# Two scans, then two gates: the order of VectorE's work in a selective-scan step

## Chip, cores and metric

The kernel runs on one core of a Trainium2 chip. The metric is the device time of one execution in microseconds; the median of three runs before the change is 5415.38 us (5413.15 to 5421.7). A core has five engines that run side by side, each taking its own instructions strictly in order and waiting on semaphores for the others: TensorE (PE, matmuls and transposes), VectorE (DVE), ScalarE (ACT), GpSimd (POOL) and SyncE (SP, which gives out most of the transfers here).

## What is computed

Sixteen sequences of 512 positions and 256 features go through a bidirectional selective state-space layer (a Mamba block), a layer norm, a mixture of soft experts and another layer norm. The part that matters here is the recurrence, which runs forward and backward, for 512 channels and 16 states each:

```python
def _selective_scan(u, dt, A, B, C, D, reverse=False):
    dA = jnp.einsum('bld,dn->bldn', dt, A)
    dB_u = jnp.einsum('bld,bld,bln->bldn', dt, u, B)
    ...
    dA_shift = jnp.pad(dA[:, 1:], ((0, 0), (0, 1), (0, 0), (0, 0)))
    dA_cum = jnp.exp(jnp.flip(jnp.cumsum(jnp.flip(dA_shift, 1), 1), 1))
    xs = jnp.cumsum(dB_u * dA_cum, 1) / (dA_cum + 1e-12)
    y = jnp.einsum('bldn,bln->bld', xs, C)
    ...
    return y + u * D
```

The kernel writes `xs` as a recurrence h[t] = exp(dt[t] A) h[t-1] + (dt u B)[t], times a factor that stands for the 1e-12 in the denominator, 0.5 (1 + tanh(...)). The product with C and the sum over states follow; the halves are taken into the weights beforehand.

## The kernel before

Channels lie on the 128 partitions in four chunks, the 512 positions along the free dimension. For each sequence `scan_part` (L392) is called four times: forward and backward, each for two of the four chunks. Within a call a loop runs over pairs of states (n = 0, 2, ..., 14) and the two chunks of the call. One turn of the inner loop is called a step here; there are 16 in a call and 1024 in all. A step does the following:

- SyncE loads `bs` and `cs`, the B and C rows of the two states, broadcast to all partitions (L416, L417, once for both chunks).
- GpSimd multiplies `du` by `bs` into `db` (L427), for both states at once.
- ScalarE computes the decay of each state with an exp (L444) and its factor `th` with a tanh (L446). The decay goes into a PSUM bank of its own, called `h`, which the scan then overwrites with its result.
- VectorE runs the recurrence of each state with a scan (L450 forward, L452 backward), and forms the gate (L455) `hg = (th + 1) * h` for each state.
- GpSimd multiplies both states' `hg` by `cs` in one instruction (L456).
- TensorE transposes `hg` and adds it up in the accumulator `acc` (L371), two steps later.

In 256 of the steps (n = 4 and 12) the second state's input comes from TensorE instead (`by_diagonal`, L405): a matmul puts it into a bank of the common PSUM pool, called `hd`, and the decay goes to an SBUF tile `dec`. The scan then overwrites `hd`. Such steps are called single here, the other 768 double.

Buffers set how far an engine may run ahead: `db` has three, `hg` four, `th` three, and the PSUM pool of `h` three banks (L97). So the exp of a state waits for the gate of the state three before it, which is the last reader of that bank; `th` has the same depth. A db product waits for the scans of the step three before it.

Besides the steps, generators give out pieces of other work: preparation of the next sequence, projections, norms, the experts of sequences already scanned. `beside_scan` (L541) takes some pieces at the end of each step. They use all engines; a piece is often a short run of VectorE and ScalarE instructions.

The order on each engine is not simply the order of the program text. A planner (the framework's) keeps its own clock and gives each engine, of the instructions it takes to be ready, the one that comes first in the program. `late(...)` pins an instruction behind the one written before it on its engine; most pieces of other work begin with such an instruction, while scans, gates, exps and tanhs are not pinned. The order so found is fixed in the built program.

Of the kernel before, what the change touches and what calls it, by code (L numbers as in the profile page):

```python
# [12 lines left out]
ALU = mybir.AluOpType  # L13
# [42 lines left out]
def seq_layers(tc, ident, neghalf, a, out):  # L56
# [20 lines left out]
    nc = tc.nc  # L77
    nb = a["x"].shape[0]
    with ExitStack() as ctx:
# [27 lines left out]
        def bank(name):  # L107
            count[0] += 1
            if tail and count[0] % 8 >= 3:
                return tail[0].tile([P, 512], F32, tag="tps", name=name)  # L110
            return ps.tile([P, 512], F32, tag="mps", name=name)
# [15 lines left out]
        def late(ins):  # L127

            return tc.keep_in_program_order(ins)
# [212 lines left out]
        def turn_pair(b, r, p, v):  # L342

            yield 2
            pts = []
            for c in (2 * p, 2 * p + 1):
                pt = bank(f"pdu_{b}_{r}_{c}")
                for lc in range(NL):
                    s = slice(lc * P, (lc + 1) * P)
                    nc.tensor.transpose(pt[:, s], v[c][2][:, s], ident)  # L350
                pts.append((c, pt))
            yield HOLD
            for c, pt in pts:
                duT = p4.tile([P, L], F32, tag="duT", name=f"duT_{b}_{r}_{c}", bufs=2)
                late(nc.scalar.copy(duT, pt))
                v[c].append(duT)
# [4 lines left out]
        def add_up(depth):  # L361
            while len(pending) > depth:
                first, unit, last, c, hc, accs, w, u, name, done = pending.pop(0)
                if first:
                    accs[c] = ps_acc.tile([P, L], F32, tag="acc", name=name)

                    late(nc.tensor.matmul(accs[c], zeros[:, :P], zeros, start=True, stop=False))
                for j in range(2):
                    for lc in range(NL):
                        s = slice(lc * P, (lc + 1) * P)  # L370
                        ins = nc.tensor.matmul(  # L371
                            accs[c][:, s],
                            hc[:, j, s],
                            ident,
                            is_transpose=True,
                            start=False,
                            stop=(last and j == 1 and lc == NL - 1),
                        )
                        if j == lc == 0:
                            late(ins)  # L380
                if unit:
                    for lc in range(NL):
                        s = slice(lc * P, (lc + 1) * P)
                        nc.tensor.matmul(accs[c][:, s], u[:, c, s], w["diagD"][:, c, :], start=False, stop=False)
                if last:
                    evictions.append(partial(done, c))

        def evict():
            while evictions:
                evictions.pop(0)()  # L390

        def scan_part(b, r, p, v, accs, done, then):  # L392

            prep.drain()
            prep.gens += [[1, g] for g in [turn_pair(b, r, p, v)] + then]
            w = side[r]
            made = {}

            def by_diagonal(n, c):

                diags.append(count[0])
                made[n, c] = h = bank(f"hd_{b}_{r}_{n}_{c}")
                for lc in range(NL):
                    s = slice(lc * P, (lc + 1) * P)
                    ins = nc.tensor.matmul(h[:, s], v[c][3][:, s], dg[:, s], start=True, stop=True)  # L405
                    if lc == 0:
                        late(ins)

            chunks = (2 * p, 2 * p + 1)
            for n in range(0, NS, 2):  # L410
                q = f"{b}_{r}_{p}_{n}"
                k = 1 if n + 1 in DIAG else 2

                bs = p4.tile([P, 2, L], F32, tag="bs", name=f"bs_{q}")
                cs = p4.tile([P, 2, L], F32, tag="cs", name=f"cs_{q}")
                nc.sync.dma_start(bs[:, :k, :], v["bc"][0, n : n + k, :].unsqueeze(0).to_broadcast([P, k, L]))  # L416
                nc.sync.dma_start(cs, v["bc"][1, n : n + 2, :].unsqueeze(0).to_broadcast([P, 2, L]))  # L417
                if n + 3 in DIAG:
                    dg = p4.tile([P, L], F32, tag="dg", name=f"dg_{q}", bufs=1)
                    nc.sync.dma_start(  # L420
                        dg.rearrange("p (l s) -> p l s", l=NL),
                        diag_dram[r, DIAG.index(n + 3), :, : P * P].rearrange("l (p s) -> p l s", p=P),
                    )
                for c in chunks:
                    dt, rr, du = v[c][:3]
                    db = p4.tile([P, 2, L], F32, tag="db", name=f"db_{q}_{c}")
                    nc.gpsimd.tensor_tensor(  # L427
                        db[:, :k, :], du.unsqueeze(1).to_broadcast([P, k, L]), bs[:, :k, :], ALU.mult
                    )
                    hg = p4.tile([P, 2, L], F32, tag="hg", name=f"hg_{q}_{c}", bufs=4)  # L430
                    hs = {}
                    for j in range(2):
                        if j < k:
                            dec = h = ps_h.tile([P, L], F32, tag="h", name=f"h_{q}_{c}_{j}")
                            hs[j] = (h, dec, db[:, j, :])
                        else:
                            h = made.pop((n + j, c))
                            dec = p4.tile([P, L], F32, tag="dec", name=f"dec_{q}_{c}", bufs=2)
                            hs[j] = (h, dec, h)

                    ths = {}
                    for j in range(2) if k == 2 else (1, 0):
                        s = slice(n + j, n + j + 1)
                        nc.scalar.activation(hs[j][1], dt, AF.Exp, scale=w["A"][:, c, s])  # L444
                        ths[j] = p4.tile([P, L], F32, tag="th", name=f"th_{q}_{c}_{j}")
                        nc.scalar.activation(ths[j], rr, AF.Tanh, bias=LN_1E12 / 2, scale=w["Ah"][:, c, s])  # L446
                    for j in range(2):
                        (h, dec, add), th = hs[j], ths[j]
                        if r == 0:
                            nc.vector.tensor_tensor_scan(h, dec, add, 0.0, ALU.mult, ALU.add)  # L450
                        else:
                            nc.vector.tensor_tensor_scan(  # L452
                                h[:, ::-1], dec[:, ::-1], add[:, ::-1], 0.0, ALU.mult, ALU.add
                            )
                        nc.vector.scalar_tensor_tensor(hg[:, j, :], th, 1.0, h, ALU.add, ALU.mult)  # L455
                    nc.gpsimd.tensor_tensor(hg, hg, cs, ALU.mult)  # L456
                    pending.append(
                        (r == n == 0, n == 0, r == 1 and n == NS - 2, c, hg, accs, w, v["u"], f"acc_{q}_{c}", done)
                    )
                    evict()  # L460

                    nxt_n = n if c == chunks[0] else n + 2
                    if nxt_n + 1 in DIAG:
                        for x in sides:
                            x.take_up()
                        by_diagonal(nxt_n + 1, chunks[1] if c == chunks[0] else chunks[0])
                    beside_scan()
                    if k == 1:
                        diags.pop(0)
                    add_up(2)  # L470
# [70 lines left out]
        def beside_scan():  # L541
            for x in sides:
                x.take_up()
            prep.piece()
            for x in (front, back) if front.credit > back.credit else (back, front):
                x.paced_piece(gaps=not hurry)
# [549 lines left out]
```

## Time and profile before

| | us |
|---|---|
| median of three runs | 5415.38 |
| the profiled execution | 5411.23 |
| its span in the trace | 5409.4 |
| busy: GpSimd, VectorE, TensorE matmul, ScalarE | 4732, 4560, 4331, 4087 |
| VectorE: scans (L450, L452) with h | 2144 in 1792 |
| VectorE: scans with hd | 312 in 256 |
| VectorE: gates (L455) | 1359 in 2048 |
| GpSimd: db (L427), hg (L456) | 2144, 2421 |
| ScalarE waits for a gate: L446, L444 | 331, 218 |

How to read the views. The page's first part gives each engine's busy time; the second cuts the span into 40 slices with the busy share of each in tenths. The groups list instructions by line and shape: out<-in, count, then total busy time, mean length in ns, then the idle time of the engine just before them and what ended most of it. A line of the waits names who waited, for whom, the total, the number of waits and the longest. A line of the timeline is a start, a length, the engine, the line and the tiles, with xN where N instructions in a row are merged. Recorded lengths of neighbours on one engine can overlap a little, so the distance between starts (the pitch) is what adds up: 1.13 us for a scan followed by something that doesn't wait for it, 0.59 us for a gate.

### The profile page before, as it was taken

To read this page: it belongs to the slowest core of one execution; us is meant where nothing else is said; L and a number is where in the kernel's file an instruction comes from. 1 tells how busy PE (TensorE), PEld (TensorE's weight loads), DVE (VectorE), ACT (ScalarE), POOL (GpSimd) and SP (SyncE) were. 2 spreads that over 40 slices of the span, in tenths; PEclk is the share of its full clock that TensorE was granted. 3 is DMA by queue.
4 is the path that set the end of the run, shared out by engine and by line. 5 is a ranking of instruction groups with operands and counts; after the bars stand their busy time and mean duration, and the time that the engine had idled before them with its cause. 6 is when DMAs were issued, how large, how long until landed. Compare 5 with 4: busy or idle time off the path is not lost. (4 is left out here: it accounts for less than half of the span.)

```text
span 5409.4 us, 73721 instructions
## 1 busy us (share of the span) xinstructions
PE 4331.1 (80%) x24144; PEld 3390.0 (63%) x24145; DVE 4559.7 (84%) x6276; ACT 4087.2 (76%) x6515; POOL 4732.1 (87%) x2537
## 2 busy tenths in 40 slices
PE   5656666898888978788888977889787897888889
PEld 3445555676666666677656765667656776667657
DVE  7888988889898899888998888988899889988722
ACT  6677777787888778887877887788788887877641
POOL 6999999999999899998999989998999989988600
PEclk7778778898899988899888989899889998989999
DMA  4334333575446644566446754467444764457436
GB/s 137 131 117 137 125 129 131 189 230 159 156 142 212 225 149 148 158 223 213 131 144 194 232 170 153 132 212 232 149 149 146 225 224 134 145 179 234 126 103 188
DMA packets 595236, 907.73 MB, mean 168 GB/s; under 512 B 78082, under 2 KB 384898, under 8 KB 594852
## 3 DMA queue, kind: packets, MB, share of 16 engines
q1 hardware_dynamic: 521156, 859.87, 49.5%
q10 hardware_dynamic: 73696, 43.14, 2.8%
q8 instruction: 192, 3.15, 0.2%
q14 instruction: 192, 1.57, 0.1%
HBM read 840.86 MB, written 62.01 MB: 167 GB/s over the span
## 5 line engine op out<-in xcount | busy, mean ns | idle before, releaser
L456 POOL TENSOR_TENSOR hg<-hg,cs 128x1024 f32<-128x1024 f32 x1024 | 2420.8, 2368 | 128.1 <-DVE hg L455 110.0
L427 POOL TENSOR_TENSOR db<-du,bs 128x1024 f32<-128x1024 f32 (+1 forms) x1024 | 2144.4, 2098 | 232.3 <-DVE h L450 84.7
L371 PE MATMUL acc<-ident,hg 128*128 128x128 f32 x8192 | 1179.3, 295 | 203.3 <-POOL hg L456 181.6
L455 DVE SCALAR_TENSOR_TENSOR hg<-th,h 128x512 f32<-128x512 f32 x1792 | 1185.8, 678 | 177.2 <-PE acc L371 90.4
L371 PEld LDWEIGHTS acc<-ident,hg 128*128 128x128 f32 x8192 | 1044.9, 154 | 390.8 <-POOL hg L456 240.9
L452 DVE TENSOR_TENSOR_SCAN h<-h,db 128x512 f32<-128x512 f32 x896 | 1072.8, 1218 | 112.2 <-ACT h L444 107.5
L450 DVE TENSOR_TENSOR_SCAN h<-h,db 128x512 f32<-128x512 f32 x896 | 1071.1, 1217 | 48.8 <-ACT h L444 45.7
L446 ACT ACTIVATE th<-rr,Ah_f 128x512 f32<-128x512 f32 x1024 | 725.0, 714 | 186.3 <-DVE hg L455 183.1
L446 ACT ACTIVATE th<-rr,Ah_b 128x512 f32<-128x512 f32 x1024 | 721.5, 712 | 155.2 <-DVE hg L455 147.7
L444 ACT ACTIVATE h<-dt,A_f 128x512 f32<-128x512 f32 x896 | 608.2, 680 | 117.5 <-DVE hg L455 112.6
L444 ACT ACTIVATE h<-dt,A_b 128x512 f32<-128x512 f32 x896 | 608.6, 681 | 108.8 <-DVE hg L455 105.1
L687 PE MATMUL pl<-x2T,seT 128*128 128x512 f32 x512 | 299.1, 715 | 78.7 <-DVE hg L455 37.4
L405 PE MATMUL hd<-dg,duT 128*128 128x128 f32 x2048 | 305.6, 298 | 32.7 <-ACT yt L627 13.5
L830 PEld LDWEIGHTS pg<-st,Wg 128*128 128x128 f32 x2048 | 244.8, 196 | 106.2 <-issue 85.0
L405 PEld LDWEIGHTS hd<-dg,duT 128*128 128x128 f32 x2048 | 283.1, 214 | 38.4 <-ACT yt L627 15.7
L806 PE MATMUL peo<-Wd,ht 128*128 128x256 f32 x1024 | 257.0, 407 | 55.6 <-DVE rr L337 38.6
L779 PE MATMUL pu<-st,Wu 128*128 128x128 f32 x2048 | 254.5, 283 | 50.1 <-DMA Wu<-in_Wu_dram 32.7
L962 PE MATMUL cpo<-ceo,ct 128*128 128x256 f32 x1024 | 254.8, 407 | 46.9 <-DVE rr L337 39.9
L779 PEld LDWEIGHTS pu<-st,Wu 128*128 128x128 f32 x2048 | 244.9, 198 | 61.5 <-DVE h L452 24.2
L830 PE MATMUL pg<-st,Wg 128*128 128x128 f32 x2048 | 269.9, 286 | 4.1 <-DMA Wg<-in_Wg_dram 3.1
L884 PE MATMUL cl<-seT,cx 128*128 128x512 f32 x512 | 244.7, 617 | 32.5 <-DVE res L272 12.3
L806 PEld LDWEIGHTS peo<-Wd,ht 128*128 128x128 f32 x1024 | 205.3, 206 | 97.7 <-DVE rr L337 41.2
(154 smaller groups left out, 6654.8 us busy)
## 6 DMA issues: line engine op xcount, KB each, us to landing
cs<-bc SPq DMA_DIRECT2D x512, 512.0 KB, 3.9
bs<-bc SPq DMA_DIRECT2D x384, 512.0 KB, 5.1
Wg<-in_Wg_dram SPq DMA_DIRECT2D x128, 512.0 KB, 6.0
Wu<-in_Wu_dram SPq DMA_DIRECT2D x128, 512.0 KB, 6.0
Wd<-in_Wd_dram SPq DMA_DIRECT2D x128, 512.0 KB, 5.5
dg<-diag_dram SPq DMA_DIRECT2D x128, 256.0 KB, 4.2
bs<-bc SPq DMA_DIRECT2D x128, 256.0 KB, 3.6
x<-in_x_dram SPq DMA_DIRECT2D x32, 512.0 KB, 6.3
```

The source lines that it names most:

```text
L371: ins = nc.tensor.matmul(accs[c][:, s], hc[:, j, s], ident, is_transpose=True, start=False, stop=(last and j == 1 and lc == NL - 1),)
L405: ins = nc.tensor.matmul(h[:, s], v[c][3][:, s], dg[:, s], start=True, stop=True)
L427: nc.gpsimd.tensor_tensor(db[:, :k, :], du.unsqueeze(1).to_broadcast([P, k, L]), bs[:, :k, :], ALU.mult)
L444: nc.scalar.activation(hs[j][1], dt, AF.Exp, scale=w["A"][:, c, s])
L446: nc.scalar.activation(ths[j], rr, AF.Tanh, bias=LN_1E12 / 2, scale=w["Ah"][:, c, s])
L450: nc.vector.tensor_tensor_scan(h, dec, add, 0.0, ALU.mult, ALU.add)
L452: nc.vector.tensor_tensor_scan(h[:, ::-1], dec[:, ::-1], add[:, ::-1], 0.0, ALU.mult, ALU.add)
L455: nc.vector.scalar_tensor_tensor(hg[:, j, :], th, 1.0, h, ALU.add, ALU.mult)
L456: nc.gpsimd.tensor_tensor(hg, hg, cs, ALU.mult)
L779: nc.tensor.matmul(pu[:, fc * P : (fc + 1) * P], got["Wu", e][:, k, fc * P : (fc + 1) * P], st[:, k, :, j * SL : (j + 1) * SL], start=(k = ...
L806: nc.tensor.matmul(po[:, j * DM : (j + 1) * DM], ht[:, fc, :], got["Wd", e0 + j][:, fc, :], start=(fc == 0), stop=(fc == NF - 1),)
L830: nc.tensor.matmul(pg[:, fc * P : (fc + 1) * P], got["Wg", e][:, k, fc * P : (fc + 1) * P], st[:, k, :, j * SL : (j + 1) * SL], start=Fals ...
```

## The change

The loop that gave out scan and gate of each state in turn is split into two loops: both scans first, then both gates. The operations, their operands and buffers are the same.

```diff
                     for j in range(2):
-                        (h, dec, add), th = hs[j], ths[j]
+                        h, dec, add = hs[j]
                         if r == 0:
                             nc.vector.tensor_tensor_scan(h, dec, add, 0.0, ALU.mult, ALU.add)
                         else:
                             nc.vector.tensor_tensor_scan(
                                 h[:, ::-1], dec[:, ::-1], add[:, ::-1], 0.0, ALU.mult, ALU.add
                             )
-                        nc.vector.scalar_tensor_tensor(hg[:, j, :], th, 1.0, h, ALU.add, ALU.mult)
+                    for j in range(2):
+                        nc.vector.scalar_tensor_tensor(hg[:, j, :], ths[j], 1.0, hs[j][0], ALU.add, ALU.mult)
                     nc.gpsimd.tensor_tensor(hg, hg, cs, ALU.mult)
```

## The prediction

> **What bounds the kernel now.** I read the page's busy line and slices first, then its costliest groups, then the waits of GpSimd and VectorE between 300 and 4950 us (the part with the steps in full swing), and last VectorE's timeline.
>
> ```profile
> span 5409.4 us, 73721 instructions
> PE 4331.1 (80%) x24144; PEld 3390.0 (63%) x24145; DVE 4559.7 (84%) x6276; ACT 4087.2 (76%) x6515; POOL 4732.1 (87%) x2537
> ...
> DVE  7888988889898899888998888988899889988722
> ...
> POOL 6999999999999899998999989998999989988600
> ```
>
> GpSimd (POOL) is busiest, and its last slices are empty: the last step's product ends at 5132 us. Then comes a tail of 277 us without steps, in which the change has nothing to move.
>
> ```profile
> L456 POOL TENSOR_TENSOR hg<-hg,cs 128x1024 f32<-128x1024 f32 x1024 | 2420.8, 2368 | 128.1 <-DVE hg L455 110.0
> L427 POOL TENSOR_TENSOR db<-du,bs 128x1024 f32<-128x1024 f32 (+1 forms) x1024 | 2144.4, 2098 | 232.3 <-DVE h L450 84.7
> ...
> L455 DVE SCALAR_TENSOR_TENSOR hg<-th,h 128x512 f32<-128x512 f32 x1792 | 1185.8, 678 | 177.2 <-PE acc L371 90.4
> ...
> L452 DVE TENSOR_TENSOR_SCAN h<-h,db 128x512 f32<-128x512 f32 x896 | 1072.8, 1218 | 112.2 <-ACT h L444 107.5
> L450 DVE TENSOR_TENSOR_SCAN h<-h,db 128x512 f32<-128x512 f32 x896 | 1071.1, 1217 | 48.8 <-ACT h L444 45.7
> ```
>
> A step (1024 of them) costs GpSimd 2.37 + 2.10 = 4.46 us; with its other work 4732 / 1024 = 4.62. VectorE's two scans and two gates are 3.8 us, its other work brings 4560 / 1024 = 4.45. Two engines of nearly equal load, so the busier one still waits for the other:
>
> ```profile
> POOL hg L456 <- DVE hg L455: 79.4, 40, 6.3
> POOL db L427 <- DVE h L450: 75.2, 49, 6.6
> POOL db L427 <- issue: 69.2, 33, 3.2
> POOL db L427 <- DVE h L452: 57.2, 34, 6.3
> ```
>
> GpSimd is idle for 326 of these 4650 us, and 212 of that is VectorE being late, for a gate (79) or a scan (132). The scan waits are the slot of db: it has three buffers, and in the trace product db of step i+3 stands ahead of product hg of step i. So GpSimd needs step i's second scan one db product (2.4 us) before it needs step i's second gate. VectorE's own stalls:
>
> ```profile
> DVE h L452 <- ACT h L444: 95.7, 86, 6.2
> DVE hg L455 <- PE acc L371: 78.5, 74, 4.2
> DVE hd L452 <- PE hd L405: 62.8, 45, 8.0
> ```
>
> And its order in the timeline (start, length, engine, line):
>
> ```profile
> 1375.97 2.34 DVE L452 TENSOR_TENSOR_SCAN h<-h,db 128x512 f32<-128x512 f32 x2
> 1378.22 1.26 DVE L455 SCALAR_TENSOR_TENSOR hg<-th,h 128x512 f32<-128x512 f32 x2
> 1379.40 1.22 DVE L452 TENSOR_TENSOR_SCAN h<-h,db 128x512 f32<-128x512 f32 x1
> 1380.76 0.69 DVE L455 SCALAR_TENSOR_TENSOR hg<-th,h 128x512 f32<-128x512 f32 x1
> 1381.36 1.23 DVE L452 TENSOR_TENSOR_SCAN h<-h,db 128x512 f32<-128x512 f32 x1
> 1382.69 0.69 DVE L455 SCALAR_TENSOR_TENSOR hg<-th,h 128x512 f32<-128x512 f32 x1
> ```
>
> The first two rows are one step given out scan, scan, gate, gate: 3.43 us to the next start. The other four are a step in the written order: 3.89 us to 1383.29, where the next row starts. So the planner already emits both orders. Numbering scans and gates by step over the whole timeline: of the 768 steps with two recurrences ("double"), 376 have both scans first and 392 the first gate ahead of the second scan; of the 256 steps with one state from TensorE ("single"), 152 have the gate ahead. At most 544 steps can change.
>
> **What the Trainium skill says.** "VectorE: DVE Perf Modes", section "The DRAIN you can't avoid", says that a chain of vector operations with a semaphore after each took as long as one without, while a same-engine read of what was just written does need a semaphore. "Perfetto Trace Analysis", section "DVE / Act Engine Instruction", says that the recorded window ends with the write acknowledgement, that the semaphore travels after it, and that an unheld successor may start fetching before it. This trace sides with the second: the 427 gates directly behind their own scan start 0.104 us (median) after its recorded end, the other 1621 start 0.084 us before the end of what precedes them. A gate behind its own scan therefore costs 0.19 us. "SBUF — State Buffer", section "SBUF: two separate sides", has VectorE contend with a GpSimd operation reading SBUF where it has two SBUF inputs; scans and gates read one operand from PSUM, and gates keep to 649 to 691 ns, so I give reordering no price there.
>
> **The change part by part.** No instruction, transfer or buffer is added or removed; the two gates' places in the program change, and with them the planner's preference when a gate and a scan are both ready. SP's and GpSimd's queues are given the same work in the same order.
> (a) Gate behind its own scan: 427 x 0.19 = 81 us of VectorE time at most. Where the second scan isn't ready when the first ends, the gate will go first as now. In the 154 double steps with the first gate directly behind its scan, the second decay (L444) had ended before the first scan in 122. I take 60% as removed: 49 us. VectorE time reaches the span only where GpSimd waits for it. I take 0.4, between none (GpSimd the bound throughout) and all; this is a choice, not a reading. Worth 19 us.
> (b) The second scan ends a gate's pitch earlier, 0.59 us. GpSimd's wait for the last scan before a db product stands in the timeline 127 times in gate-first steps. With each cut by at most 0.59 us that is 66 us; counting runs of stalls no more than three steps apart once, 37 us. An earlier scan inside a run only helps once, so I take the 37, times 60%: 22 us.
> (c) A gate that waits (for TensorE to free hg, or for its tanh) no longer has a scan behind it. First gates with a wait over 0.2 us in gate-first steps: 58, and capped at a scan's pitch of 1.13 us they hold 48 us. Times 60%, times 0.4: 12 us.
> (d) A scan that is moved up but late now has a gate behind it that could have filled its wait. If every gate-first step flipped, 76 double and 75 single steps would wait, and what the gate's 0.59 us filled adds up to 36 + 37 = 73 us. The planner moves only what it thinks ready; I take a fifth, times 0.4: 6 us lost.
> (e) The first gate comes 1.13 us later, and holds its PSUM bank (three of them) and its tanh buffer as long. ScalarE's next exp and tanh queue behind that wait. 358 of the 1792 exps already start right as a bank comes free. 74 of these follow a first gate that would move, and in each the scan comes later than the exp by more than the shift, even with (b) on top: nothing lost, by that count. Lost from the other side: ScalarE is 79% busy here and a delay can meet a burst of its other work; all scan waits that now trace to a bank sum to 4 us. I take 5, with 15 as the far end.
> Sum: 19 + 22 + 12 - 6 - 5 = 42 us. On the profiled execution's 5411 that is 5369; the median of the runs shown lies 4 us higher, so 5373. What is late next is GpSimd's wait for the second gate (79 us), which the change leaves in place, and its waits on issue (69).
> At the ends: all of (a) to (c) at full pass, without clustering, is 81 + 66 + 48 = 195 us; nothing flipped is 0; (d) alone at full is +73.
>
> **The rivals.**
> No change in effect: the planner chooses by readiness, 520 steps of 1024 already have the new order, and the rest keep the old because the second scan comes late. For it: ScalarE stalls and PE hd waits exist. Against it: 238 double steps have something else between first scan and first gate, so both were often ready when the gate was chosen. Time 5415, within 5404 to 5426.
> Larger gain: VectorE, not GpSimd, sets the pace in most stretches, so pass-on is nearer 0.8 and flips nearer 0.8. (a) 52, (b) 30, (c) 31, less 10: 103 us, 5312. For it: GpSimd's waits name VectorE most. Against it: GpSimd's slices are at 9 almost throughout.
> Slower: the scan moved up is late on the chip. Place: second scans that wait for an exp (L444) or for TensorE's hd (L405), with a ready gate now held behind them, its bank, tanh buffer and GpSimd's hg with it. Price 73 us at most, half of it reaching the span 36 us, less 10 us of (a): 5441. It decides if more than about half of the 151 late second scans are moved up: then (d) passes the gain of (b). For it: VectorE's largest stalls are just these scans. Against it: in double steps that already have both scans first, second-scan waits over 0.1 us sum to only 26 us; in single ones, though, to 99 us.
>
> **How the numbers follow.** Forecast (gain of 12 to 80 us) 0.52, larger gain 0.12, no effect 0.14, slower 0.22. A re-made plan also shifts where other work falls, which can tip a small gain either way; that is in these shares. About 0.2% (11 us) is what a measurement of this kernel tells from no change. Faster 0.64, same 0.14, slower 0.22. The likeliest case alone spans 5335 to 5403; the range 5312 to 5445 runs from the larger gain to the slower case, and leaves a tenth at each end.
>
> **What would show it.** Right: the share of steps with both scans first well above half, gates directly behind their own scan well under 427, GpSimd's waits for scans under 132 us, its wait for gates about the same. (d) or the slower rival: longer VectorE waits on L444 and L405 than 137 and 92 us. (e): more ScalarE waits on gates than 299 + 190 us with scans starved behind them. Wrong outright: the order hardly altered, or GpSimd's scan waits shortened but its gate waits grown by as much.

## The result, and the profile after

The changed kernel takes 5442.68 us (median of five runs, 5438.91 to 5449.91), the kernel before 5416.6 beside it: 1.0048 times as long, with a 95% interval of 1.0034 to 1.0063. That is 26 us slower, where 42 us faster was forecast. The profiled execution took 5442.68 us, with a span of 5440.9.

The page of the changed kernel, its span and busy lines:

```profile
span 5440.9 us, 73750 instructions
...
PE 4338.3 (80%) x24144; PEld 3385.6 (62%) x24145; DVE 4559.8 (84%) x6276; ACT 4088.4 (75%) x6517; POOL 4735.5 (87%) x2537
```

No engine has more to do: VectorE's busy time is the same to 0.1 us, GpSimd's within 3.4, ScalarE's within 1.2, TensorE's (whose ends are modelled) within 7.2. The span is longer because the engines wait more. The same groups as before (line numbers from 456 on stand one higher, and L456 is now the gate):

```profile
L457 POOL TENSOR_TENSOR hg<-hg,cs 128x1024 f32<-128x1024 f32 x1024 | 2418.0, 2365 | 93.6 <-DVE hg L456 79.6
L427 POOL TENSOR_TENSOR db<-du,bs 128x1024 f32<-128x1024 f32 (+1 forms) x1024 | 2143.1, 2096 | 284.9 <-DVE h L450 100.1
...
L452 DVE TENSOR_TENSOR_SCAN h<-h,db 128x512 f32<-128x512 f32 x896 | 1077.9, 1223 | 116.5 <-ACT h L444 112.2
L450 DVE TENSOR_TENSOR_SCAN h<-h,db 128x512 f32<-128x512 f32 x896 | 1078.2, 1222 | 112.7 <-ACT h L444 107.5
```

One row changed in kind: the idle time before the forward scans (L450) went from 48.8 to 112.7 us, nearly all of it waiting for an exp (L444). The backward scans (L452) stand at 116.5 against 112.2. The waits of GpSimd between 300 and 4950 us (who waits, for whom, total, times, longest):

```profile
POOL db L427 <- issue: 89.4, 40, 4.0
POOL db L427 <- DVE h L450: 86.1, 37, 3.8
POOL db L427 <- DVE h L452: 63.5, 44, 6.3
POOL hg L457 <- DVE hg L456: 45.5, 35, 8.1
```

The waits of VectorE in the same stretch:

```profile
DVE h L452 <- ACT h L444: 100.8, 90, 5.5
DVE h L450 <- ACT h L444: 98.6, 66, 4.6
DVE hd L452 <- PE hd L405: 56.3, 38, 7.9
```

and the one row of the kernel before that changed most:

```profile
DVE h L450 <- ACT h L444: 41.8, 27, 3.4
```

GpSimd now waits less for a gate (45.5 us, before 79.4) and more for a scan (150, before 132) and on issue (89, before 69). VectorE's wait of forward scans for an exp went from 41.8 us in 27 waits to 98.6 in 66.

Numbering the scans and gates by step over the whole timeline, as the prediction did: steps with the gate ahead of the second scan went from 544 to 331 (224 turned round, 11 turned the other way). Of the 224 only 18 had a second scan whose input came after the first gate's start before, and these 18 scans waited 14.4 us in all before and 17.1 in the changed kernel. Gates directly behind their own scan went from 427 to 416 only. TensorE's order is the same instruction for instruction; VectorE's differs at 1502 of 6276 places, ScalarE's at 1421 of 6076 that the program gives it, GpSimd's at 125, SyncE's at 191.

**Where the time came from.** A sequence has four calls of `scan_part`, called parts here. By the end of each part's last hg product, as a mean over the sequences 2 to 14 (counted from 0), in us:

| | forward, chunks 0 and 1 | backward, 0 and 1 | forward, 2 and 3 | backward, 2 and 3 | sum |
|---|---|---|---|---|---|
| before | 79.06 | 79.83 | 78.51 | 79.03 | 316.43 |
| changed | 80.82 | 78.10 | 80.41 | 78.90 | 318.23 |

The forward parts lost 1.8 and 1.9 us a sequence, the first backward part gained 1.7. Within the first forward part the largest change by position is one scan: the second scan of step 7 (n = 6, second chunk; steps of a sequence count from 0) waited 0.0 us a sequence before and 2.45 after. ScalarE's timeline around that step in sequence 5, in the kernel before (start, length, engine, line):

```profile
1610.52 0.67 ACT L444 ACTIVATE h<-dt,A_f 128x512 f32<-128x512 f32 x1
...
1611.18 0.72 ACT L446 ACTIVATE th<-rr,Ah_f 128x512 f32<-128x512 f32 x1
1611.92 1.28 ACT L259 ACT_TABLE_LOAD   x1
1613.21 1.92 ACT L259 ACTIVATE xb<-xb 128x2048 f32<-128x2048 f32 x1
1615.14 1.28 ACT L847 ACT_TABLE_LOAD   x1
```

and in the changed kernel:

```profile
1614.94 1.28 ACT L259 ACT_TABLE_LOAD   x1
1616.24 1.91 ACT L259 ACTIVATE xb<-xb 128x2048 f32<-128x2048 f32 x1
1618.17 1.28 ACT L444 ACT_TABLE_LOAD   x1
1619.46 0.69 ACT L444 ACTIVATE h<-dt,A_f 128x512 f32<-128x512 f32 x1
...
1620.82 1.28 ACT L848 ACT_TABLE_LOAD   x1
```

The `h` exp at 1610.52 is the decay of step 7's second state. Before, it ran ahead of the long Silu of xb (L259). Now it stands behind the Silu with a table load on each side of it, a block of 4.5 us (1614.94 to 1619.46). Where a Gelu follows, as here, the exp between Silu and Gelu needs one load more; around this step five sequences have one load more than before. The exp is behind the Silu in 15 of 16 sequences, before in none. VectorE in the changed kernel over the same stretch:

```profile
1610.43 1.23 DVE L450 TENSOR_TENSOR_SCAN h<-h,db 128x512 f32<-128x512 f32 x1
1611.56 0.73 DVE L199 SCALAR_TENSOR_TENSOR pb<-xf,cw_b,pb 128x510 f32<-128x510 f32 x1
1612.19 1.23 DVE L450 TENSOR_TENSOR_SCAN h<-h,db 128x512 f32<-128x512 f32 x1
1613.33 0.72 DVE L199 SCALAR_TENSOR_TENSOR xb<-xf,cw_b,pb 128x509 f32<-128x509 f32 x1
1613.96 1.28 DVE L456 SCALAR_TENSOR_TENSOR hg<-th,h 128x512 f32<-128x512 f32 x2
1615.16 1.23 DVE L450 TENSOR_TENSOR_SCAN h<-h,db 128x512 f32<-128x512 f32 x1
1616.52 0.69 DVE L456 SCALAR_TENSOR_TENSOR hg<-th,h 128x512 f32<-128x512 f32 x1
1620.19 1.23 DVE L450 TENSOR_TENSOR_SCAN h<-h,db 128x512 f32<-128x512 f32 x1 [2.98 <-ACT h L444]
```

The first and third rows are the two scans of step 6, the fifth its two gates, the last two scans step 7's. The L199 rows are taps of a convolution, a piece of other work. With three banks, step 7's second exp gets the bank that step 6's first gate gives back. That gate starts 3.53 us after its scan (1613.96 less 1610.43). In the kernel before they are 1.77 us apart:

```profile
1607.73 1.23 DVE L450 TENSOR_TENSOR_SCAN h<-h,db 128x512 f32<-128x512 f32 x1
1608.87 0.73 DVE L199 SCALAR_TENSOR_TENSOR pb<-xf,cw_b,pb 128x510 f32<-128x510 f32 x1
1609.50 0.68 DVE L455 SCALAR_TENSOR_TENSOR hg<-th,h 128x512 f32<-128x512 f32 x1
```

The bank comes free at about 1614.6 here, so on the chip the exp could still have gone ahead of the Silu's load at 1614.94; the order fixed at build time does not allow it. Before, step 7's second scan had room: it started 2.99 to 3.35 us after its exp had ended, in every sequence. So a gate that is 1.76 us later would not by itself have made this scan wait; the block of 4.5 us does. The wait reaches GpSimd, whose next db product in the changed kernel needs that scan:

```profile
1621.50 2.36 POOL L427 TENSOR_TENSOR db<-du,bs 128x1024 f32<-128x1024 f32 x1 [3.31 <-DVE h L450]
```

This is the theory for the experiments: the loss is step 6's first gate, its bank, and an exp that the re-made order of ScalarE puts behind a Silu. The rivals: late second scans moved up (the prediction's slower case), and a general cost of the new order spread evenly over all steps.

### The profile page after: what moved, and what is told of

It reads as the page before. It is cut to its first block, busy times and chain, and to the rows that moved or that the text cites. A ratio compares the mean times of both kernels' runs of the same rounds, so it can differ in the third digit from the quotient of the medians.

```text
span 5440.9 us, 73750 instructions
## 1 busy us (share of the span) xinstructions
PE 4338.3 (80%) x24144; PEld 3385.6 (62%) x24145; DVE 4559.8 (84%) x6276; ACT 4088.4 (75%) x6517; POOL 4735.5 (87%) x2537
## 5 line engine op out<-in xcount | busy, mean ns | idle before, releaser
L456 DVE SCALAR_TENSOR_TENSOR hg<-th,h 128x512 f32<-128x512 f32 x1792 | 1180.7, 682 | 164.5 <-PE acc L371 93.5
L452 DVE TENSOR_TENSOR_SCAN h<-h,db 128x512 f32<-128x512 f32 x896 | 1077.9, 1223 | 116.5 <-ACT h L444 112.2
L450 DVE TENSOR_TENSOR_SCAN h<-h,db 128x512 f32<-128x512 f32 x896 | 1078.2, 1222 | 112.7 <-ACT h L444 107.5
L444 ACT ACTIVATE h<-dt,A_b 128x512 f32<-128x512 f32 x896 | 610.4, 683 | 111.3 <-DVE hg L456 109.1
L444 ACT ACTIVATE h<-dt,A_f 128x512 f32<-128x512 f32 x896 | 610.0, 682 | 95.7 <-DVE hg L456 90.9
L831 PEld LDWEIGHTS pg<-st,Wg 128*128 128x128 f32 x2048 | 258.6, 205 | 116.1 <-issue 83.8
L405 PE MATMUL hd<-dg,duT 128*128 128x128 f32 x2048 | 300.0, 294 | 24.4 <-DVE rr L337 6.4
L405 PEld LDWEIGHTS hd<-dg,duT 128*128 128x128 f32 x2048 | 278.1, 211 | 30.0 <-ACT yt L628 7.8
L831 PE MATMUL pg<-st,Wg 128*128 128x128 f32 x2048 | 285.0, 296 | 12.3 <-DMA Wg<-in_Wg_dram 8.8
```

The lines of the kernel that those rows point to most:

```text
L452: nc.vector.tensor_tensor_scan(h[:, ::-1], dec[:, ::-1], add[:, ::-1], 0.0, ALU.mult, ALU.add)
L456: nc.vector.scalar_tensor_tensor(hg[:, j, :], ths[j], 1.0, hs[j][0], ALU.add, ALU.mult)
L831: nc.tensor.matmul(pg[:, fc * P : (fc + 1) * P], got["Wg", e][:, k, fc * P : (fc + 1) * P], st[:, k, :, j * SL : (j + 1) * SL], start=Fals ...
```

## Experiments

Each ratio is against the kernel before, run beside it on the same chip, with its 95% interval.

| label | what differs from the kernel before | median us | ratio |
|---|---|---|---|
| e1_swap_ready | 393 swaps held on VectorE, second scan ready | 5403.95 | 0.9980 [0.9972, 0.9988] |
| e2_swap_all | all 544 swaps held | 5519.79 | 1.0196 [1.0182, 1.0209] |
| e3_vector_order | VectorE's order of the changed kernel | 5427.61 | 1.0024 [1.0017, 1.0031] |
| e4_vector_scalar_order | VectorE's and ScalarE's order of it | 5443.91 | 1.0055 [1.0043, 1.0067] |
| e5_only_step6 | 16 swaps, step 6 only | 5416.07 | 1.0007 [1.0001, 1.0014] |
| e6_ready_not6 | the swaps of e1 without step 6's 16 | 5383.71 | 0.9948 [0.9936, 0.9960] |
| e7_source_not6 | changed source, step 6 as before | 5390.94 | 0.9966 [0.9953, 0.9978] |
| e8_after_mended6 | all orders of the changed kernel, two places mended | 5429.64 | 1.0034 [1.0022, 1.0046] |
| e9_decay_in_sbuf | changed source, one decay outside the bank | 5420.88 | 1.0016 [1.0009, 1.0022] |
| e10_forward_only | new loops in forward parts only | 5431.70 | 1.0038 [1.0024, 1.0051] |
| e11_backward_only | new loops in backward parts only | 5377.10 | 0.9932 [0.9919, 0.9945] |
| e12_not6_exp_before_gelu | orders of e7, one exp moved in five sequences | 5375.36 | 0.9939 [0.9927, 0.9951] |

**Holding an order.** In e1 to e6, e8 and e12 the source is that of the kernel before, and every engine's order is held by dependencies that set an order and no semaphore. The traces agree that nothing else moves: in e5 TensorE and ScalarE run in the order of the kernel before, row for row, and VectorE's order differs at 48 places, three for each of its 16 swaps.

```diff
     seq_layers(tc, ident, neghalf, a, out)
+    for engine, order in ORDERS.items():
+        ins = [i for i in tc.nc.cur_bb.bb.instructions if str(i.engine) == "EngineType." + engine]
+        for p, q in zip(order, order[1:]):
+            tc.add_manual_dep(
+                ins[q], ins[p].name,
+                mybir.DependencyInfo(mybir.DependencyClass.NoSync, mybir.DependencyReason.DATA),
+                reason="order",
+            )
```

**e1: the new order where the second scan was ready.** On VectorE the second scan is put ahead of the first gate in the 393 steps (of 544) whose second scan had its input by the time the first gate started, in the trace of before; all else keeps before's order.

> The order of every engine's instructions is held to that of the kernel before; only on VectorE, in the 393 gate-first steps whose second scan had its input in the profile of before by the time the first gate started, the second scan is put directly ahead of the first gate. If my steps (a) to (c) are sound and the loss lies in what the planner re-made elsewhere (theory A): 5360 to 5400 us, GpSimd's waits for scans well under 157 us. If the order scan, scan, gate, gate is itself worth nothing or harmful even where the scan is ready (theory B): 5410 to 5440.

0.20% faster. Gates directly behind their own scan fell from 427 to 124. GpSimd's waits for scans fell from 132 to 109 us, about what step (b) of the prediction had (22), but its wait for gates rose by 18 us:

```profile
POOL hg L456 <- DVE hg L455: 97.3, 61, 7.8
POOL db L427 <- DVE h L450: 64.9, 36, 3.7
...
POOL db L427 <- DVE h L452: 44.2, 41, 4.6
```

So the idea works where it is applied to ready scans, and 18 of the 23 us come back as a later gate.

**e2: all of them.** The remaining 151 steps, whose second scan was late by that measure, are swapped as well.

> As the run before it, but the second scan is put ahead of the first gate in all 544 gate-first steps, also in the 151 whose second scan was late. Theory A: about as fast as with the 393 alone, within 15 us of it and under 5416. The slower rival of the prediction (late second scans hold ready gates behind them): 20 to 60 us above the run with the 393 alone, and at or above 5425.

2% slower, 116 us above e1, 0.77 us for each of the 151 steps. In the swapped steps second scans now wait 239.5 us in 173 waits. The mechanism of the prediction's slower rival is real and dearer than its 73 us, but the planner did not do this: it turned round 18 such steps, whose second scans wait 2.7 us longer in all (17.1 against 14.4).

**e3 and e4: which engine's order carries the loss.** e3 takes only VectorE's list from the changed kernel, e4 VectorE's and ScalarE's.

> VectorE's whole order is that of the changed kernel, ScalarE, GpSimd, TensorE and SyncE are held to the order of before. Theory A (ScalarE's re-made order loses the time): 5385 to 5415. Theory B (VectorE's own order loses it): 5432 to 5450. Third theory (the two orders only fit together, a mixture stalls both): above 5450.

> VectorE and ScalarE both in the order of the changed kernel, GpSimd and SyncE in the order of before. Theories A and B: 5435 to 5448, as the changed kernel. If GpSimd's or SyncE's re-made order carries the loss instead: 5400 to 5420.

e3 is 0.24% slower (13 us by the ratio), e4 0.55%, as much as the changed kernel. GpSimd's and SyncE's orders carry nothing that can be seen; the loss is VectorE's and ScalarE's, about half each in this order of adding them. ScalarE in e3 at the same place, where the exp still stands ahead of the Silu:

```profile
1616.97 0.69 ACT L444 ACTIVATE h<-dt,A_f 128x512 f32<-128x512 f32 x1 [1.38 <-DVE hg L455]
...
1618.37 1.28 ACT L259 ACT_TABLE_LOAD   x1
```

The exp waits 1.38 us for the gate, and the Silu block with all that follows starts later by that. With ScalarE's old order the late bank shows as a wait. Step 7's second scan then waits for nothing, but the exps of step 8 come behind the delayed block, and step 8's two scans wait 2.64 and 1.35 us a sequence, before 1.43 and 0.10. With ScalarE's new order there is no wait for the bank, the exp is late by a whole block instead, and step 7's second scan waits. In the traces the first forward part takes 81.90 us a sequence in e3 and 80.76 in e4 (before 79.06), the second one 79.38 and 81.52 (before 78.51). So the late gate costs the first forward part about as much with the exp ahead of the Silu as behind it, and what ScalarE's new order adds lies in the second forward part. The traced execution of e3 is the slowest of its 22, 15 us over their median, so its parts are somewhat long.

**e5 and e6: step 6 alone, and all but step 6.** e5 swaps only the 16 steps 6 of the first forward part, e6 is e1 without them (377 swaps).

> Every engine's order is that of the kernel before, except that VectorE takes the second scan ahead of the first gate in 16 steps of 1024: step 6 (counted from 0) of the first forward part of each sequence, where the second scan was ready. Theory A2 (that gate frees the PSUM bank for the second decay of step 7, behind which ScalarE's Silu block waits, so VectorE runs dry after it): 5425 to 5445, with VectorE's waits for the decays of steps 7 and 8 up by 1.2 to 2.5 us per sequence. Rival (the loss is spread over the re-made orders and no single step matters): 5408 to 5418.

> The swaps of the first experiment (second scan ahead of the first gate where it was ready) without those 16: 377 swaps. Theory A2: 5380 to 5398, faster than with the 16. Rival: 5399 to 5410, as with them.

Alone, the 16 swaps cost 0.07%, 4 us; the expected size was missed by far. Left out of e1 they are worth 0.32%: e6 is 0.52% faster than before, e1 0.20%. So the theory has the right place, but 16 moved instructions have no fixed price. Step 8's first scan waits 2.10 us a sequence in e5 and 2.18 in e1, against 1.43 in before and 1.53 in e6, so the delay arrives in both. That the rest of e5 has the slack to absorb it, and the tighter e1 has not, is the likely reading and not shown.

**e7: the changed source, with step 6 exempted.** The planner is free.

```diff
+                        if r == p == 0 and n == 6 and c == chunks[0]:
+                            nc.vector.scalar_tensor_tensor(hg[:, j, :], ths[j], 1.0, h, ALU.add, ALU.mult)
-                    for j in range(2):
+                    for j in range(0 if r == p == 0 and n == 6 and c == chunks[0] else 2):
                         nc.vector.scalar_tensor_tensor(hg[:, j, :], ths[j], 1.0, hs[j][0], ALU.add, ALU.mult)
```

> The changed source, but in step 6 of the first forward part scan and gate stay in turn; the planner orders everything anew. Theory A2: 5395 to 5418. Rival: 5430 to 5450, as the changed kernel.

0.34% faster than before, and by the two ratios 0.82% or 44 us below the changed kernel, with one step of 64 in its old order. The exp is ahead of the Silu in all 16 sequences. GpSimd's and VectorE's orders still differ from before's at 94 and 1293 places, ScalarE's at 1192: a re-made plan as such is not what costs. By the parts (table below), 2.2 of the 2.9 us a sequence that e7 is shorter than the changed kernel lie in the first forward part.

**e8: the changed kernel's own orders, mended by hand.** All lists are those of the changed kernel; step 6's first gate goes ahead of its second scan (16 moves on VectorE), and step 7's exp and tanh ahead of the Silu (30 moves on ScalarE).

> Every engine's order is that of the changed kernel, except that in step 6 of each sequence's first forward part VectorE takes the first gate ahead of the second scan (16 moves), and ScalarE takes the second exp and tanh of step 7 ahead of the Silu. Theory A2: 5395 to 5418. Rival: 5430 to 5450.

1.0034 against 1.0048: about a third of the loss regained, and as the two intervals overlap the share is uncertain. The wait of step 7's second scan is gone (2.45 to 0 us a sequence), but step 8's first scan waits 3.24 us where it waited 1.43 in before. Step 7's exp now starts 1.5 to 2.5 us after the gate that frees its bank has ended, in before 0.03 to 0.34: the work around it was ordered for the late exp. A miss, and the second sign, after e5, that the moves do not add up.

**e9: the bank taken out of the chain.** Both scans stay ahead of both gates in all steps, step 6 too. Only one decay is written elsewhere, so that it no longer waits for step 6's first gate.

```diff
                             dec = h = ps_h.tile([P, L], F32, tag="h", name=f"h_{q}_{c}_{j}")
+                            if (r, p, n, c, j) == (0, 0, 6, 1, 1):
+                                dec = p4.tile([P, L], F32, tag="dec", name=f"dec_{q}_{c}", bufs=2)
                             hs[j] = (h, dec, db[:, j, :])
```

> The changed kernel, with one decay moved: in the first forward part the second state of the step with n = 6 and the second chunk (step 7) writes its exp into an SBUF tile dec instead of the PSUM bank h; the scan still writes the bank. Nothing is computed differently, and both scans stay ahead of both gates everywhere, step 6 included. In this program's fixed order the second exp of step 7 is ahead of the Silu of xb in 16 of 16 sequences (changed kernel: behind it in 15). If the loss is that this exp waits for the bank which the first gate of step 6 gives back late: 5380 to 5405, near the kernel that exempted step 6 (5390.9). If the delayed gates themselves, the tanh buffers or the rest of the re-made plan carry it: 5425 to 5445.

5420.88 us lies between the two expectations. The first forward part went from 80.82 us in the changed kernel to 79.32 (79.06 before): 1.50 of its 1.76 us are back, with the gates and the tanh buffers as late as in the changed kernel and only the bank taken out (the planner then puts this exp ahead of the Silu in all 16 sequences). The edit brought a cost of its own, which was not foreseen. Its 16 scans, in the groups with different forms kept apart:

```profile
L452 DVE TENSOR_TENSOR_SCAN h<-dec,db 128x512 f32<-128x512 f32 x16 | 56.2, 3515 | 0.0
```

VectorE's timeline in one sequence, the second row being such a scan:

```profile
1944.36 1.22 DVE L452 TENSOR_TENSOR_SCAN h<-h,db 128x512 f32<-128x512 f32 x1
1945.49 3.03 DVE L452 TENSOR_TENSOR_SCAN h<-dec,db 128x512 f32<-128x512 f32 x1
```

GpSimd's timeline beside it (L459 is this kernel's hg product):

```profile
1945.08 2.36 POOL L459 TENSOR_TENSOR hg<-hg,cs 128x1024 f32<-128x1024 f32 x1
1948.66 2.35 POOL L427 TENSOR_TENSOR db<-du,bs 128x1024 f32<-128x1024 f32 x1 [1.22 <-issue]
```

These scans read both inputs from SBUF. The one shown starts while GpSimd's product runs, ends 1.08 us after that product's end (1948.52 against 1947.44), and GpSimd's next instruction starts only when it is done. At 3515 ns against 1218 they took 37 us more of VectorE, and GpSimd was idle for 1.17 to 1.23 us behind 15 of them, 18 us in all. Without it e9 would stand near 5400, an estimate from these rows; it was not tried.

**e10 and e11: forward parts only, backward parts only.** The exemption of e7 with the condition `r == 1` keeps backward parts in the old order, with `r == 0` the forward ones.

> The new loops in the two forward parts of a sequence only; backward parts keep scan, gate, scan, gate. The second exp of step 7 is behind the Silu in 15 of 16 sequences, as in the changed kernel. If the loss sits in the first forward part: +1.8 us a sequence there, about nothing elsewhere, so 5425 to 5445. If it is spread over all steps: near 5428 at most, and if the backward steps carry it, 5415 or less.

> The new loops in the two backward parts only. The changed kernel's backward parts were 1.73 and 0.13 us a sequence shorter than before's, and none of the forward part's late exps is in this program. Loss in the forward parts: 16 x 1.86 = 30 us less than before, 5380 to 5400. Loss spread over all steps: 5420 to 5430.

Forward only is 0.38% slower, with the exp behind the Silu in 15 of 16 sequences and the second scan of step 7 waiting 2.43 us a sequence. Backward only is 0.68% faster, more than expected. This excludes a cost of the new order spread evenly over all steps. The two do not add up to the changed kernel (about -16 us against +26): with both, the plan has a second bad place that neither has alone. It is the subject of e12 and accounts for a part of the difference; the rest stays open.

**e12: the second place.** In e7 five sequences (in the changed kernel six) have, at the first step of the second forward part, an exp between two Gelus. ScalarE in e7, sequence 5:

```profile
1726.31 0.60 ACT L850 ACTIVATE ht<-pg 128x512 f32<-128x512 f32 x1
1726.93 1.28 ACT L444 ACT_TABLE_LOAD   x1
1728.22 0.69 ACT L444 ACTIVATE h<-dt,A_f 128x512 f32<-128x512 f32 x1
1728.93 1.28 ACT L853 ACT_TABLE_LOAD   x1
1730.22 0.60 ACT L853 ACTIVATE ht<-pg 128x512 f32<-128x512 f32 x1
1730.72 0.71 ACT L446 ACTIVATE th<-rr,Ah_f 128x512 f32<-128x512 f32 x1
```

In e12 that exp is moved up by one place in these five sequences, all other orders being e7's:

```profile
1727.62 0.67 ACT L444 ACTIVATE h<-dt,A_f 128x512 f32<-128x512 f32 x1
1728.31 1.28 ACT L847 ACT_TABLE_LOAD   x1
1729.61 0.60 ACT L847 ACTIVATE ht<-pg 128x512 f32<-128x512 f32 x1
1730.10 0.59 ACT L850 ACTIVATE ht<-pg 128x512 f32<-128x512 f32 x1
```

(The two Gelus are L850 and L853 in e7, L847 and L850 in e12.)

> The program of the kernel that exempted step 6, its orders held on every engine, with one exp in each of five sequences moved one place up on ScalarE: the second exp of the second forward part's first step, which stood between two Gelus (table loads on both sides), now stands ahead of both. Two table loads of 1.28 us less in five sequences. If they lie on the path: up to 5 x 2.6 = 13 us less than that kernel, 5376 to 5388. If they are covered: 5391, and the second forward part's +1.4 us a sequence has another cause.

0.27% or 15 us below e7 by the ratios (about 9 us either way), for five moved instructions, and just under the lower end of what was expected. Ten table loads of 1.28 us are 12.8, which agrees with their lying on the path in full. The second forward part went from 79.90 to 78.78 us a sequence (78.51 before), the other three parts stayed within 0.1. In just the five sequences with the move it is 1.9 to 3.8 us shorter, in every other one within 0.6. The tanh at 1730.72 follows a Gelu without a load, so of a step's activations it is only the exps that cost loads there.

Such exps are not new, however. The kernel before has 15 of them, and so has the changed kernel. At the first step of the first backward part, in sequence 5 of the kernel before, ScalarE's timeline has:

```profile
1655.17 1.28 ACT L444 ACT_TABLE_LOAD   x1
1656.47 0.69 ACT L444 ACTIVATE h<-dt,A_b 128x512 f32<-128x512 f32 x1
1657.18 1.28 ACT L850 ACT_TABLE_LOAD   x1
```

This exp stands between two Gelus in six sequences before and in none of the changed kernel, where the exp of the second forward part's first step does in the same six. In these six sequences the first backward parts together gained 19.4 us and the second forward parts lost 17.5. About half of that gain is also there in e3, where ScalarE keeps its old order (9.9 us), so what the move cost on balance is not shown. e12 prices the place in the plan of e7, not as a part of the 26 us. e10, e11 and e12 have nine such exps each.

Time by part of the sequence, in us, for the kernels with a free planner and e12:

| | fwd 0, 1 | bwd 0, 1 | fwd 2, 3 | bwd 2, 3 | sum |
|---|---|---|---|---|---|
| e7 | 78.64 | 77.93 | 79.90 | 78.85 | 315.32 |
| e9 | 79.32 | 78.13 | 80.51 | 78.99 | 316.94 |
| e10 | 81.56 | 78.40 | 78.89 | 79.70 | 318.56 |
| e11 | 78.79 | 78.44 | 78.18 | 77.98 | 313.39 |
| e12 | 78.55 | 77.85 | 78.78 | 78.81 | 314.00 |

e10 shows a limit of this table: its backward part lost its text's change and is still 1.4 us shorter than before's. Work that a slow part has already done may be missing from the next, so only sums over neighbours can be read as gains. The traced execution of e10 is moreover the slowest of its six, 17 us over their median. e11 and e12 are both faster than the kernel before and the changed one, and not to be told apart.

## Why the prediction was wrong

**The step that failed is (e)**, the first gate that holds its bank. It was priced at 5 us with 15 as the far end. With the changed source, exempting step 6 is worth 44 us (e7). Moving the exp out from among the Gelus is worth another 15 (e12), though the kernel before has as many such exps elsewhere. It failed in three ways. The delay of the gate is 1.76 us at the decisive place, not 1.13, since a tap of other work (L199) stands between the scans too. The count of exps that start as a bank comes free was right on the old order of ScalarE, but the planner decides that order afresh: in the changed kernel the exp stands behind a Silu with two table loads, and a scan that had 3 us of room waits 2.45 us a sequence. And the count looked only at each exp's own scan. Where ScalarE's order is held (e3, e5) that scan indeed waits for nothing, but what stands behind the exp on the queue, the Silu block and the exps of step 8, is delayed with it, and step 8's first scan already waited 1.43 us before. "A delay can meet a burst of its other work" named the case, and sized it as a mean. "The Trainium skill", page "ScalarE: Activation LUTs", section "Table sets: the hidden batching unit", says to batch activations by set; this case's 15 us for five exps agrees, and the prediction had not asked where a table switch was next in the queue.

**Its sign was wrong too.** The prediction would have taken more ScalarE waits on gates than 299 + 190 us as evidence for (e). They fell, to 278 + 167 (tanh and exp). At the decisive place the late bank was turned into an order, and then ScalarE shows no wait for it; what is left is VectorE's wait for the exp (L450 on L444, 41.8 to 98.6 us).

**(a)** hardly happened: 427 gates behind their own scan became 416, not 171. e1 shows that 303 could go; the planner left them.

**(b)** was right in size where swaps were held (GpSimd's scan waits down 23 us in e1), and 18 us of that came back as gate waits. In the changed kernel scan waits rose. In e12 they are 139 us, no better than before's 132, and the gain is in the gate waits (79 to 48) and on issue (69 to 58); by this path (b) is not confirmed.

**(c)** was not separated from the rest by any run.

**(d)** was right: the planner turned round 18 late steps, and their second scans wait 2.7 us longer in all. e2 prices the other course at 116 us instead of 73.

**The sum without (e)** was 47 us. The cleanest measure of it is e6, where ScalarE keeps the order of before and 377 ready scans are moved up: 0.52% or 28 us. e11 and e12, free of both bad places, gained 0.68% and 0.61%, 37 and 33 us. These are not gains of the forecast's parts alone: e11 has the new loops in half of the steps only, and e11 and e12 have 325 and 321 table loads where the kernel before has 337. At 1.28 us each that is up to 15 and 20 us, an estimate that takes all of them to lie on the path; the forecast had no such term. So a gain was there, smaller than the sum where it is measured cleanly. That the slower rival's 5441 comes close to 5442.68 is chance: its mechanism did not act. Of its two signs VectorE's wait on L444 did grow, for another reason, while its waits on L405 stayed at 92 us (L450 and L452 together).

**What stays open.** Why the same 16 moves are worth 4, 17 or 44 us in different surroundings (e5, e6 against e1, e7) is understood only in outline: slack elsewhere and a planner that answers. The second forward part also lost 0.8 to 1.8 us in sequences 6, 8, 10, 12 and 14, which have no exp among Gelus there; no run separates that. e8 shows that mending two places in a finished order need not mend the whole. Exempting step 6 in the source is one remedy; a fourth bank for `h` was not tried.

## What to carry to other kernels

When an instruction that gives back a buffer is moved later, find who takes that buffer next, and then what stands behind it on that engine's queue. The slack of the one reader is not enough: the delay passes on to all that queues behind, or, where a planner fixes the orders, the late instruction goes behind a long block and is late by the block's length with its table loads. In the second case the lateness need not show as a wait on the resource, so compare the orders of the engines by position before and after, and look for the one operation that changed sides with a long one. Test such a place by exempting it alone in the source, since an order mended by hand afterwards regained about a third here.

## What was not expected of the hardware

A scan with both inputs in SBUF met GpSimd's multiplications and took 3515 ns in the mean (16 of them, 1607 to 6612) instead of 1218 with its decay in PSUM. "The Trainium skill", page "SBUF — State Buffer", section "Who interferes with whom", says that a VectorE instruction with two SBUF inputs contends with a GpSimd instruction that reads SBUF, and that the one that comes second blocks until the first is done; the rows of e9 agree, to the 1.08 us that the scan needs once GpSimd's product has ended. In three of the 16 (5.8 to 6.6 us) the scan ended 1.09 us after the last of three GpSimd products back to back, so two further ones had gone ahead of it. It is also a reason to keep the decays in the banks whose number caused the loss.

A table switch took 1.28 us for the load and 1.30 to the start of the next activation (1614.94 to 1616.24 in the changed kernel), between exp, Silu and Gelu alike.
